# Indirect gathers on GpSimd: a fixed order, and a wait for the predecessor's landing before every fourth

## The chip, the cores and the metric

The kernel runs on one core of one Trainium2 chip. The metric is the device time of one execution in microseconds, as the median of plain executions (without the profiler). Three such runs of the kernel before gave 609.22, 614.84 and 617.77 us.

## The reference

Two layers of a graph network over 4096 nodes with 64 features, with a 0/1 adjacency matrix of 4096 x 4096 whose entries are 1 with probability 0.00195, about eight in a row. Cut to what matters:

```python
# layer 0: hyperbolic aggregation over a node's neighbours
h = max(layernorm(x), 0)
w = adj / max(adj.sum(axis=1), 1e-8)
log_ij = logmap(h_i, h_j)             # Poincare ball: Mobius addition, arctanh of its norm
agg = einsum("ij,ijc->ic", w, log_ij)
x = x + expmap(0, agg @ W0 + b0)      # a tanh of the norm
# layer 1: neighbours weighted by their place in the row
h = max(layernorm(x), 0)
rank = cumsum(adj != 0, axis=1); deg = rank[:, -1:]
k = min(deg, 100); pos = rank - (deg - k)
wt = mask * where(pos > 0, 0.5 ** (k - pos), 0)
x = x + wt @ (h @ W1) + b1
```

Layer 0 needs a function of both nodes for each edge, so the features of each neighbour have to be fetched; layer 1 is a matrix product whose weights fall by half with each neighbour counted from the end of the row.

## The kernel before

The 4096 rows are 32 blocks of 128 (one row a partition), in four quarters of eight blocks. The whole adjacency matrix is read once, in 256 loads of 128 x 512 numbers (256 KB each) on the queue of SyncE (`load`, line 795). TensorE transposes each piece (line 799), ScalarE writes it as an 8-bit mask into SBUF (line 801), and TensorE multiplies the mask with powers of two to pack 16 columns into one word (`pack`, line 822).

From the packed words VectorE finds the column numbers of a row's neighbours: `search` (lines 843 and 845) takes the largest 24 words of a row, `ell_lists` (line 866) turns the first eight into the row numbers `ell_i`. What doesn't fit into eight goes to a short list for the whole block, made by `tail_split`, `tail_first` and `tail_second`, which ends in `tail_i` (line 973): two entries for each partition and block.

Layer 0 is done on 16 units of two row blocks. A table in HBM, `tab_d`, has one row of 65 numbers (260 bytes) for each node: a scale and its 64 features. It is written once near the start (line 760). For a unit, `gather` (line 987) issues 16 indirect DMAs for two blocks of eight neighbours, and, for 12 of the units, 4 or 6 more for `tail_i`. One such DMA (line 995, called a gather below) takes 128 row numbers, one for each partition, and fetches 128 table rows into one of the 22 columns of the buffer `g`. There are 256 + 64 = 320 gathers. They are issued by GpSimd, which does nothing else after the first microseconds. The buffer `g` comes from the pool `gp`, which has two: the gathers of a unit can start when the unit two before it has finished with its own.

What uses a unit's buffer, in this order: `differ` subtracts the row's own features (VectorE, lines 1038, 1045 and 1053) and squares (ScalarE, line 1060, back into `g`); `weigh` sums the squares (VectorE, line 1072, the last reader of `g`) and computes the weight of each edge in small operations on VectorE and ScalarE; `total` adds up the weighted differences (line 1117 and following, with TensorE products at line 1107 for tail entries). When the units of a group of row blocks are done, `middle` (four steps) does layer 0's product, tanh and layer norm, and layer 1's product `h @ W1`, into `sup`. Groups are 8, 8, 8, 6 and 2 blocks.

Layer 1's weights come from `ranks` (lines 1223 to 1231): two matrix products on the mask count the neighbours to the right, and ScalarE's Exp turns the counts into powers of two, in place of the mask. `collect` (line 1246) multiplies these weights with `sup`, and VectorE reduces and adds the result (lines 1254 and 1258). `write` sends the output out.

All of this is written as a plan: each piece is given a due time by hand, and the pieces are handed to a scheduler in that order. Gathers are planned at 1.26 us each:

```python
took = 1.26 * (E2 + (u["tail"][1] * TB if u["tail"] else 0))
t = start + took
at(u_fetch, fetch, u)
at(start, gather, u)
```

From the due times as priorities, and from modelled times at which inputs become ready, the scheduler lays out one fixed list of instructions for each engine when the program is built. It also adds the semaphore waits. An engine works its list in order: an instruction that waits holds up those behind it. The gathers count their landing on eight semaphores, in turn; a gather thus waits for the one eight before it. At the end a flag tells whether any list was too short; a second, dense path would then run (it doesn't with these inputs).

Of the kernel before, what the change touches and what calls it, by code (L numbers as in the profile page):

```python
# [53 lines left out]
SUB = 40  # L54
REST = 64
TB = 2
MAXT = 3
ROW1 = 4096.0

# [479 lines left out]
def kernel(  # L539
# [27 lines left out]
    nc = tc.nc  # L567
# [8 lines left out]
    GB = P // GRP  # L576
    NSL = 2 * ELL + MAXT * TB
    SB = 4
# [12 lines left out]
    def by_rows(t):  # L591
        return t.rearrange("(b p) c -> p b c", p=P)

    with ExitStack() as fast:
# [26 lines left out]
        rest = const.tile([P, P], BF16, name="rest_b")  # L621
# [34 lines left out]
        ell_i = const.tile([P, NB, ELL], I32, name="ell_i")  # L656
        tail_i = const.tile([P, NB, TB], I32, name="tail_i")
        tail_r = const.tile([P, NB, TB], F32, name="tail_r")
        acc = const.tile([P, NB, D], F32, name="acc")
# [120 lines left out]

        EARLY = {"middle":30,"search":30,"fetch_words":30,"tail_rows":30,"differ":30,"weigh":30,"total":30,"total_tail":30,"ell_lists":30,"tail_split":20,"tail_first":20,"tail_second":20,"gather":30,"fetch":30}
        st = {}

        groups = [(0, 8), (8, 8), (16, 8), (24, 6), (30, 2)]

# [157 lines left out]
        def tail_second(q):  # L943
# [21 lines left out]
            nc.vector.transpose(lt, tb)  # L965
            lv = lt.rearrange("p (s t n b) -> p s n b t", s=2, t=TB, n=2)
            li = lst.tile([P, QB, TB], I32, name="li")
            for n in range(2):
# [9 lines left out]
        def fetch(u):  # L978
# [3 lines left out]
            if u["tail"]:  # L982
                t0, nt = u["tail"]
                u["hr"] = hr = blk.tile([P, MAXT, 3 * DT], BF16, name="hr")
                nc.scalar.dma_start(out=hr[:, 0:nt, :], in_=by_rows(hp_d)[:, t0 : t0 + nt, :])

        def gather(u):
            rb = u["ell"]
            g = u["g"] = gp.tile([P, NSL, DT], F32, name="g")
            idx = [ell_i[:, rb + b, s : s + 1] for b in range(2) for s in range(ELL)]  # L990
            if u["tail"]:
                t0, nt = u["tail"]
                idx += [tail_i[:, t0 + b, t : t + 1] for b in range(nt) for t in range(TB)]
            for k, i in enumerate(idx):
                nc.gpsimd.indirect_dma_start(  # L995
                    out=g[:, k, :],
                    out_offset=None,
                    in_=tab_d,
                    in_offset=bass.IndirectOffsetOnAxis(ap=i, axis=0),
                )  # L1000
            u["ns"] = len(idx)

        def tail_rows(u):
# [4 lines left out]
            nb = nt * TB  # L1008
            oh = u["oh"] = blk.tile([P, MAXT * TB, P], BF16, name="oh")
            row = tail_r[:, t0 : t0 + nt].rearrange("p b t -> p (b t)")  # L1010
# [5 lines left out]
            )  # L1016
            mp = ps_m.tile([P, MAXT * TB, P], BF16, name="mi")
            for k in range(nb):
                nc.tensor.transpose(mp[:, k, :], oh[:, k, :], ident_b)
            mt = blk.tile([P, MAXT * TB, P], BF16, name="mt")  # L1020
            nc.scalar.copy(mt[:, 0:nb], mp[:, 0:nb])
            sel = u["sel"] = ps_s.tile([P, MAXT * TB, DT], F32, name="sel")
            for k in range(nb):
# [280 lines left out]
        for n, u in enumerate(units):  # L1304
            lists = u["ell"] + 2 if u["ell"] < QB else (u["ell"] // 4 + 1) * 4
            start = max(t, loaded(lists - 1) + 6.0)
# [4 lines that stand above are left out]
            z = start + SH  # L1311
            u_fetch = z + 3.0
            at(z, tail_rows, u)
            at(z + 1.0, differ, u)
            at(z + 4.0, weigh, u, 0)
            at(z + 5.0, weigh, u, 1)
            at(z + 6.0, weigh, u, 2)
            at(z + 7.0, total, u)
            at(z + 8.0, total_tail, u)
            for k, (m, z0) in enumerate(todo):  # L1320
                at(max(z, TLOADED + 4.0 + 12.0 * m) + z0, middle, m, k % 4)
            todo = []
            for m, (g0, nb) in enumerate(groups):
                if u["tail"] and m not in ready and g0 + nb <= sum(u["tail"]):

                    todo += [(m, z0) for z0 in (1.5, 4.5, 5.5, 7.5)]
                    ready[m] = t + 30.0
# [69 lines left out]
```

## Time and profile before

| | |
|---|---|
| plain executions, median of three | 614.84 us (609.22 to 617.77) |
| profiled execution | 873.66 us |
| its span, first to last instruction | 871.5 us |
| gathers on GpSimd (line 995) | 320, 0.94 us each in most cases, starts 1.25 us apart in a row of them |
| first gather, last gather start | 56.9 us, 757.9 us |
| packets of the gathers' DMA queue | 10240, 8.8% of 16 DMA engines' time |
| adjacency loads | 256 of 256 KB |
| mean granted TensorE clock | 0.73 |

The profiled execution is 42% longer than the plain ones. Every time of an instruction below is from the profiled execution, and the prediction says how it gets from one to the other. In the profile's lines, L995 is line 995 of the kernel; PE is TensorE's products and PEld its weight loads, DVE is VectorE, ACT ScalarE, POOL GpSimd, SP SyncE, and a q behind an engine's name means its queue of DMA issues. "a<-b" means that tile a is computed from tile b. An arrow behind an idle time names what ended it; "issue" means that nothing in the profile explains the wait, and "remote" that a semaphore's update was seen but not whose it was.

### The profile page before, as it was taken

To read this page: it belongs to the slowest core of one execution; us is meant where nothing else is said; L and a number is where in the kernel's file an instruction comes from. 1 tells how busy PE (TensorE), PEld (TensorE's weight loads), DVE (VectorE), ACT (ScalarE), POOL (GpSimd) and SP (SyncE) were. 2 spreads that over 40 slices of the span, in tenths; PEclk is the share of its full clock that TensorE was granted. 3 is DMA by queue.
4 is the path that set the end of the run, shared out by engine and by line. 5 is a ranking of instruction groups with operands and counts; after the bars stand their busy time and mean duration, and the time that the engine had idled before them with its cause. 6 is when DMAs were issued, how large, how long until landed. Compare 5 with 4: busy or idle time off the path is not lost.

```text
span 871.5 us, 11735 instructions
## 1 busy us (share of the span) xinstructions
PE 481.0 (55%) x4170; PEld 317.3 (36%) x4170; DVE 408.2 (47%) x1494; ACT 354.1 (41%) x550; POOL 319.4 (37%) x332
## 2 busy tenths in 40 slices
PE   3654346276116628382553717655663199569894
PEld 2421124144003315151432404222422088359783
DVE  4550216356201627262542705844581054389786
ACT  3543237286006628281653806834481023022100
POOL 0035761604770441547053170555367502600000
PEclk9995557688557858586675966958695589578886
DMA  7899447387225647483563722211212100100002
GB/s 213 241 168 135 111 120 208 97 247 201 49 50 181 193 91 240 102 239 67 177 180 95 240 57 52 35 25 30 38 31 27 23 20 16 24 6 8 2 3 51
DMA packets 85590, 89.19 MB, mean 102 GB/s; under 512 B 46098, under 2 KB 47634, under 8 KB 85522
## 3 DMA queue, kind: packets, MB, share of 16 engines
q1 hardware_dynamic: 66194, 74.93, 31.6%
q0 software_dynamic: 10240, 10.67, 8.8%
q10 hardware_dynamic: 9088, 2.75, 1.4%
q8 instruction: 34, 0.56, 0.3%
q14 instruction: 34, 0.28, 0.1%
HBM read 84.12 MB, written 4.19 MB: 101 GB/s over the span
## 4 chain that ended last, share of the span: by engine, by line
PE 26%; another core or an unknown queue 22%; DMA 21%; issue 11%; DVE 10%; ACT 8%; SPq 2%; ACTq 0%; DVEq 0%
DMA a_sb<-in_adj 20%; PE a_ps L1246 8%; PE a_ps L799 5%; ACT mask L1231 3%; PE t L1227 3%; PE t L1223 3%; ACT mask L801 2%; DVE red L1254 2%; PE sel L1107 2%; PE words L1141 2%; SPq L795 1%; DVE acc L1258 1%; ACT g L1060 1%; PE o L1137 1%
## 5 line engine op out<-in xcount | busy, mean ns | idle before, releaser
L995 POOL DMA_INDIRECT g<-tab_d,ell_i x256 | 255.2, 997 | 406.2 <-DVE d L1072 124.8
L1231 ACT ACTIVATE mask<-t,w_c 128x512 fp8e5<-128x512 f32 x256 | 172.7, 691 | 205.3 <-remote 122.6
L1223 PE MATMUL t<-mask,rest_b 128*128 128x512 fp8e4 x248 | 114.3, 461 | 141.8 <-ACT mask L1231 101.7
L801 ACT ACTIVATE mask<-a_ps 128x1024 fp8e4<-128x1024 bf16 x128 | 131.2, 1028 | 138.1 <-remote 88.8
L799 PE MATMUL a_ps<-ident_b,a_sb 128*128 128x128 bf16 x1024 | 127.0, 263 | 94.6 <-DMA a_sb<-in_adj 68.5
L799 PEld LDWEIGHTS <-a_sb 128*128 128x128 bf16 x1024 | 79.8, 116 | 158.4 <-DMA a_sb<-in_adj 111.6
L1227 PE MATMUL t<-mask,before 128*128 128x512 fp8e4 x256 | 119.1, 465 | 1.8 <-issue 1.7
L1246 PE MATMUL a_ps<-sup,mask 128*128 128x192 bf16 x1024 | 109.6, 267 | 15.8 <-issue 9.8
L1246 PEld LDWEIGHTS <-mask 128*128 128x128 fp8e5 x1024 | 95.6, 106 | 29.5 <-issue 24.0
L1227 PEld LDWEIGHTS <-before 128*128 128x128 bf16 x256 | 27.4, 107 | 167.5 <-issue 165.5
L822 PE MATMUL words<-pk,mask 128*128 128x8 bf16 x1024 | 47.3, 169 | 59.7 <-issue 30.5
L822 PEld LDWEIGHTS <-mask 128*128 128x128 fp8e4 x1024 | 44.0, 104 | 92.1 <-issue 49.5
L995 POOL DMA_INDIRECT g<-tab_d,tail_i x64 | 62.4, 976 | 32.6 <-issue 18.9
L843 DVE MAX8 cand<-wsb 128x8 f32<-128x256 f32 x96 | 36.9, 416 | 68.7 <-ACT wsb L833 44.7
L1254 DVE TENSOR_REDUCE red<-a_ps 128x128 f32<-128x384 f32 x64 | 35.6, 556 | 26.2 <-PE a_ps L1246 17.9
L1223 PEld LDWEIGHTS <-rest_b 128*128 128x128 bf16 x248 | 28.0, 113 | 19.1 <-issue 10.6
L1072 DVE TENSOR_REDUCE d<-g 128x22 f32<-128x1408 f32 (+2 forms) x16 | 23.8, 1485 | 22.0 <-ACT g L1060 14.8
L1141 PE MATMUL words<-w_sb,a_sb 64*128 64x64 f32 x128 | 23.8, 339 | 17.2 <-issue 15.8
L1038 DVE TENSOR_TENSOR d<-g,hi 128x1024 f32<-128x1024 f32 x16 | 19.4, 1215 | 28.0 <-DMA g<-tab_d,ell_i 27.9
L1138 ACT COPY a_sb<-o 64x512 f32<-64x512 f32 (+1 forms) x18 | 9.5, 529 | 53.5 <-remote 18.1
L1141 PEld LDWEIGHTS words<-w_sb,a_sb 64*128 64x128 f32 x128 | 21.0, 243 | 24.1 <-issue 19.7
L1137 PE MATMUL o<-ident,y 128*64 128x128 f32 x64 | 14.2, 357 | 24.3 <-issue 12.8
(285 smaller groups left out, 535.0 us busy)
## 6 DMA issues: line engine op xcount, KB each, us to landing
a_sb<-in_adj SPq DMA_DIRECT2D x256, 256.0 KB
g<-tab_d,ell_i POOLq DMA_INDIRECT x256
hp_d<-mask SPq DMA_DIRECT2D x1, 1560.0 KB
hr<-hp_d ACTq DMA_DIRECT2D x8, 146.2 KB
tab_d<-mask SPq DMA_DIRECT2D x1, 1040.0 KB
hi<-tab_d ACTq DMA_DIRECT2D x16, 64.0 KB
g<-tab_d,tail_i POOLq DMA_INDIRECT x64
out<-acc SPq DMA_DIRECT2D x8, 128.0 KB
```

The lines of the kernel that those rows point to most:

```text
L799: nc.tensor.transpose(a_ps[:, m, k, :], upper[:, bass.ts(k, P)], ident_b)
L801: nc.scalar.activation(masks[q][:, 2 * SB * n : 2 * SB * n + 2 * SB, bass.ts(b, P)], a_ps.rearrange("p m k f -> p (m k) f"), AF.Copy, satu ...
L822: nc.tensor.matmul(words[:, rb % 2, bass.ts(j, GB)], lhsT=masks[q][:, j, bass.ts(b, P)], rhs=pk, start=False, stop=True, skip_group_check= ...
L843: nc.vector.max(out=top, in_=src)
L995: nc.gpsimd.indirect_dma_start(out=g[:, k, :], out_offset=None, in_=tab_d, in_offset=bass.IndirectOffsetOnAxis(ap=i, axis=0),)
L1072: nc.vector.tensor_reduce(d2, u["g"][:, 0:ns, 1:DT], AX.X, ALU.add)
L1141: nc.tensor.matmul(sp[:, k, :], lhsT=ht[:, bass.ts(k, P)], rhs=w_sb, start=True, stop=True)
L1223: nc.tensor.matmul(t, lhsT=rest, rhs=masks[p][:, j + 1, bass.ts(n, SW)], start=False, stop=False, skip_group_check=True,)
L1227: nc.tensor.matmul(t, lhsT=before, rhs=masks[p][:, j, bass.ts(n, SW)], start=(j == NB - 1), stop=True, skip_group_check=True,)
L1231: nc.scalar.activation(masks[p].bitcast(F8W)[:, j + 1, bass.ts(n, SW)], t, AF.Exp, bias=w_c, scale=-LN2, saturate=False,)
L1246: nc.tensor.matmul(o[:, k, :], lhsT=masks[p].bitcast(F8W)[:, b0 + j + 1, bass.ts(2 * n + k, P)], rhs=st["sup", c][:, j, :], start=(j == 0) ...
L1254: nc.vector.tensor_reduce(red, o.rearrange("p k (n c) -> p k c n", n=3), AX.X, ALU.add)
```

## The change

Each gather is tied to the one issued before it, across units. Three of four ties give an order only. The fourth, before gathers number 4, 8, 12 and so on, counted from 0 over the whole kernel, makes the gather wait until the one before it has landed in SBUF.

```diff
 TB = 2
+RUN = 4
...
         st = {}
+        runs = []
+        landed = mybir.DependencyInfo(
+            mybir.DependencyClass.Sync, mybir.DependencyReason.DATA
+        )
+        queued = mybir.DependencyInfo(
+            mybir.DependencyClass.NoSync, mybir.DependencyReason.DATA
+        )
...
             for k, i in enumerate(idx):
-                nc.gpsimd.indirect_dma_start(
+                ins = nc.gpsimd.indirect_dma_start(
                     out=g[:, k, :],
                     out_offset=None,
                     in_=tab_d,
                     in_offset=bass.IndirectOffsetOnAxis(ap=i, axis=0),
                 )
+
+                if runs:
+                    dep = landed if len(runs) % RUN == 0 else queued
+                    tc.add_manual_dep(ins.ins, runs[-1], dep, reason="rest")
+                runs.append(ins.ins.name)
             u["ns"] = len(idx)
```

`Sync` edges become semaphore waits; `NoSync` edges only fix the order in the list. Since the scheduler sees the waits when it lays out the lists, the order of instructions on the other engines can change too.

## The prediction

> **What bounds the kernel now.** I read the page first: span, busy shares, GpSimd's slices and the chain that ended last.
>
> ```profile
> span 871.5 us, 11735 instructions
> PE 481.0 (55%) x4170; PEld 317.3 (36%) x4170; DVE 408.2 (47%) x1494; ACT 354.1 (41%) x550; POOL 319.4 (37%) x332
> ...
> PE 26%; another core or an unknown queue 22%; DMA 21%; issue 11%; DVE 10%; ACT 8%; SPq 2%; ACTq 0%; DVEq 0%
> ...
> L995 POOL DMA_INDIRECT g<-tab_d,ell_i x256 | 255.2, 997 | 406.2 <-DVE d L1072 124.8
> ...
> L995 POOL DMA_INDIRECT g<-tab_d,tail_i x64 | 62.4, 976 | 32.6 <-issue 18.9
> ```
>
> No engine is full and the 320 gathers of line 995 are not on the chain. But 22% of the chain has no known releaser, and this execution took 873.7 us where plain ones took 614.8. So I asked what is different in it. Busy time by stretch (columns: length, then busy us and instructions of PE, PEld, DVE, ACT, POOL, then clock, DMA share, GB/s), cut where gathers run (205:261, 293:319) and pause:
>
> ```profile
> 172.00:205.00 33.00, 23.12 (x230) 13.33 (x230) 19.05 (x81) 25.56 (x37) 0.02 (x1) 0.81 0.76 222
> 205.00:261.00 56.00, 13.95 (x129) 7.78 (x128) 12.66 (x50) 10.61 (x14) 42.90 (x44) 0.59 0.38 85
> 261.00:293.00 32.00, 20.56 (x242) 12.90 (x241) 13.05 (x48) 23.82 (x36) 0.00 (x1) 0.80 0.65 199
> 293.00:319.00 26.00, 8.60 (x67) 4.35 (x63) 9.15 (x44) 6.37 (x11) 19.25 (x20) 0.59 0.40 94
> ...
> 759.00:871.50 112.50, 85.29 (x752) 75.39 (x751) 87.73 (x304) 14.66 (x38) 0.00 (x0) 0.76 0.06 14
> ```
>
> Under the profiler TensorE issues 230 matmuls in 33 us without gathers and 129 in 56 us beside them. The list of waits shows where ScalarE lost that time, and what GpSimd waited for (total us, times, longest):
>
> ```profile
> ACT mask L1231 <- remote: 122.6, 20, 18.8
> ACT mask L801 <- remote: 88.8, 14, 20.7
> ...
> POOL g L995 <- DVE d L1072: 124.8, 4, 41.6
> POOL g L995 <- issue: 95.6, 302, 3.9
> ...
> POOL g L995 <- DMA g<-tab_d,ell_i: 8.1, 5, 4.5
> ```
>
> With the two smaller entries of the same kind (18.1 and 14.3 us) ScalarE's waits of unknown origin sum to 243.8 us; 871.5 - 243.8 = 627.7 us, close to the plain 614.8. I read it so: most of these stalls belong to the profiled execution, and a plain one is that execution without them. Then GpSimd's 288.8 us of waiting between bursts (all its waits but issue and the first one, for tab_d) shrinks with them. GpSimd's timeline gives its pace:
>
> ```profile
> 79.15 0.94 POOL L995 DMA_INDIRECT g<-tab_d,ell_i  x1 [4.51 <-DMA g<-tab_d,ell_i]
> 82.74 0.94 POOL L995 DMA_INDIRECT g<-tab_d,ell_i  x1 [2.65 <-DMA g<-tab_d,ell_i]
> ...
> 226.36 0.94 POOL L995 DMA_INDIRECT g<-tab_d,ell_i  x1 [0.31 <-issue]
> 227.60 0.94 POOL L995 DMA_INDIRECT g<-tab_d,ell_i  x1 [0.30 <-issue]
> 228.85 0.94 POOL L995 DMA_INDIRECT g<-tab_d,tail_i  x1 [0.30 <-issue]
> ```
>
> Starts are 1.25 us apart (0.94 and 0.30), so 320 gathers are 400 us of GpSimd's time. The first starts at 56.9 us, and 112.5 us follow the last. 57 + 400 + 112.5 + 2.2 (873.7 - 871.5, outside the span) = 571.7; the plain 614.8 leaves GpSimd 43 us of waiting. By this sum the gathers pace a plain run, though the profiled chain hides it.
>
> **What the Trainium skill says.** "DMA: Bandwidth & Descriptors", section "Anatomy of one DMA — SWDGE (gpsimd) path", gives a GpSimd DMA a fixed cost of about 2.0 us, most of it the confirmation that the last byte has landed. The trace agrees: from a gather's start to the last of its recorded semaphore updates I count 2.09 us at least, 2.45 median, 3.0 mean (worst 16, while the first loads crowd the queues). "Perfetto Trace Analysis", section "Per-instruction lifecycle: what the profiler-reported window actually captures", says that such an instruction's profiled end is the end of descriptor generation and that GpSimd is better timed by the spacing of starts; hence 1.25 us and not 0.94.
>
> **The change part by part.** *Fixed order.* In the timeline the gathers already run unit by unit, 16 by ell_i and then 4 or 6 by tail_i; one place differs (18 ell_i starts from 204.98 on, before the six tail_i: two gathers of unit 5 go ahead of unit 4's tail). Swapping those costs about nothing, since unit 4's tail rows start right behind without a wait. *The ordering edges* add no instruction.
>
> *The waits.* Gathers 4, 8, ... 316 wait until the one before has landed: 79 waits. Today the gathers count on eight semaphores, 40 each, and gather n waits for gather n-8; that is almost always over (8.1 us in all, 5 times). The new wait is never over: the predecessor started only 1.25 us earlier and needs 2.45. Restart after a landing is 0.26 us (in the two rows at 79.15 and 82.74 the semaphore's last update is at 78.89 and 82.48). So each wait costs 2.45 + 0.26 - 1.25 = 1.46 us; from below, with the shortest landing, 2.09 + 0.26 - 1.25 = 1.10; from above, with the mean, 2.0. It can't be below nothing, as no landing seen is under 1.25 us. Times 79: 115 us, between 87 and 158. A run of four takes 6.5 us instead of 5.0, a unit of 22 some 8 us more.
>
> Behind a waiting gather stand only gathers. For them wait VectorE's differ (lines 1038 and 1045), then ScalarE's square (1060), VectorE's sum (1072), weigh, total, middle and, last, collect. VectorE, ScalarE and TensorE also hold loads' transposes, ranks and collects behind these in their fixed queues, so lateness spreads.
>
> *What covers it.* In the profiled execution, 288.8 us of GpSimd waits lie between bursts, so most of 115 us can hide there: 873.7 us plus 0 to 115, less whatever shorter stalls give back. In a plain run the cover is the 43 us alone, mostly waits for a free g buffer (pool gp has two), which slower gathers do absorb. With all of it: 614.8 + 115 - 43 = 687 us. None absorbed gives 730. Later gathers also leave VectorE (87.7 us busy in the last 112.5) less left over from before: with nothing left over the last unit's differ, at 787.8, would start 2.4 us after the last gather, and 86 us would follow that gather instead of 112.5; this gives 661. I take the middle of 687 and 661, 674 us. With the shortest tail and the cheapest waits, 57 + 400 + 87 + 86 + 2.2 = 632.
>
> *The rest.* Instructions of the other engines are the same, but their order is laid out at build time from modelled readiness, which the waits shift. No row prices that; I take nothing, with some 15 us either way inside the range.
>
> **Rivals.** *Hidden (no change).* The plain spacing of gathers may be less than the profiled 1.25. With 0.95 (0.30 of issue gone) gathers are 304 us, slack 139, and waits 79 x (2.45 + 0.26 - 0.95) = 139: 615 us. For it: GpSimd is not on the profiled chain. Against: each of several hundred spacings is 1.25, and all slack would have to lie where the waits fall.
>
> *Rest heals the stalls (faster).* The first stall comes some 10 us into a burst (burst from 112.06, TensorE idle from 122), as if something filled up; a pause after every fourth gather may let it drain. If a plain run keeps a share of the 243.8 us and the pauses clear it, GpSimd's own path decides: with spacing 0.95 it is 57 + 304 + 139 + 86 = 586 us. It decides only where stall time saved exceeds the waits not covered, and at 1.25 spacing the floor of 632 rules it out. For it: the threefold slowdown beside gathers. Against: 627.7 against 614.8, which leaves plain runs hardly any stall.
>
> *The waits don't do what they say:* if they were satisfied already, as the eight-semaphore waits are, 615 us; the landing times speak against it, and I count it with no change.
>
> **How the numbers follow.** Likeliest, waits on the pacing path: 0.76, 674 us, its own range 632 to 735. No change: 0.12, 615. Stalls heal: 0.12, 586. The range reaches down to 606, taking in most of no change and leaving out healing, and up to 735, with some 0.06 above. Faster by over 2% 0.12, within 2% 0.12, slower by over 2% 0.76; 2% is about what a measurement of this kernel tells from no change.
>
> **What would show it.** Right: GpSimd's timeline has groups of four starts 1.25 us apart, then a start some 2.7 us after its predecessor with a DMA of g as releaser; about 79 such waits of 1.2 to 1.7 us beyond the 0.30; plain time up by 45 to 115 us. Wrong: gaps before every fourth gather near 0.30; or plain time unchanged with the gaps there (GpSimd had slack); or, beside gathers, matmuls and GB/s near those of stretches without, and plain time down (stalls are real in plain runs, and rest clears them).

## The result, and the profile after

The changed kernel takes 761.7 us (760.1 to 765.2) against 614.84 us: 1.242 times the time before, 95% interval 1.226 to 1.257. Forecast were 674 us, 606 to 735. The direction and the place were right, the size was not. The page of the kernel after, whose profiled execution took 760.1 us, as long as its other runs:

```profile
span 758.2 us, 11815 instructions
PE 474.9 (63%) x4170; PEld 320.3 (42%) x4170; DVE 414.5 (55%) x1494; ACT 357.2 (47%) x550; POOL 331.5 (44%) x332
...
L1003 POOL DMA_INDIRECT g<-tab_d,ell_i x256 | 265.3, 1036 | 302.9 <-DMA g<-tab_d,ell_i 162.6
...
L1003 POOL DMA_INDIRECT g<-tab_d,tail_i x64 | 64.4, 1007 | 55.8 <-DMA g<-tab_d,tail_i 22.1
...
g<-tab_d,ell_i POOLq DMA_INDIRECT x256, 2.9
```

The gathers (line 1003 now) are as many as before and about as long (1.04 us in the mean for those by `ell_i`, 1.00 before). What ended GpSimd's idle time has changed: the landing of a gather instead of a result of VectorE. The last line is the median from issue to landing, 2.9 us. The list of waits (total us, times, longest):

```profile
POOL g L1003 <- DMA g<-tab_d,ell_i: 181.6, 63, 13.7
...
POOL g L1003 <- issue: 84.1, 241, 4.3
...
POOL g L1003 <- DMA g<-tab_d,tail_i: 22.1, 8, 5.5
```

There are 71 waits on a landing with 203.7 us, where there were 5 with 8.1; ScalarE's waits of unknown origin are gone from the list. GpSimd's timeline (start, length, idle before):

```profile
206.31 1.50 POOL L1003 DMA_INDIRECT g<-tab_d,ell_i  x1 [3.45 <-DMA g<-tab_d,ell_i]
208.11 0.94 POOL L1003 DMA_INDIRECT g<-tab_d,ell_i  x1 [0.30 <-issue]
209.35 0.94 POOL L1003 DMA_INDIRECT g<-tab_d,ell_i  x1 [0.30 <-issue]
210.60 0.94 POOL L1003 DMA_INDIRECT g<-tab_d,ell_i  x1 [0.30 <-issue]
214.52 0.94 POOL L1003 DMA_INDIRECT g<-tab_d,ell_i  x1 [2.98 <-DMA g<-tab_d,ell_i]
```

Groups of four as foreseen, but the start at 214.52 comes 3.92 us after its predecessor, not 2.7. Over all 79 waits that spacing is 3.89 us in the mean.

The earlier profile of the kernel before had stalls that the plain runs lacked, so one experiment took a second one (first below). Against it the whole difference can be read from GpSimd's row alone. The table splits the span of each profiled execution at the starts of the first and the last of the 320 gathers; the first column of times is the median time of the kernel, in the first row that of one execution. Two runs on the old lists, with the waits two back and with the waits on the gather itself, are not in it, since their profiled executions were over 1% longer than the median of their others.

| kernel | median us | ratio to before | to first gather | first to last | after last | span |
|---|---|---|---|---|---|---|
| before, again | 610.9 | | 55.7 | 459.2 | 93.9 | 608.8 |
| after | 761.7 | 1.242 | 55.7 | 634.2 | 68.3 | 758.2 |
| old lists, 79 waits | 816.9 | 1.315 | 57.6 | 665.2 | 92.0 | 814.8 |
| new lists, no waits | 667.6 | 1.075 | 57.2 | 529.8 | 80.0 | 667.0 |
| order only | 627.2 | 1.011 | 58.0 | 461.0 | 107.3 | 626.3 |
| old lists, four back | 628.5 | 1.012 | 57.4 | 472.3 | 94.1 | 623.8 |
| old lists, every eighth | 716.7 | 1.162 | 56.4 | 563.1 | 94.5 | 714.0 |
| old lists, first half | 721.7 | 1.170 | 57.4 | 568.5 | 93.8 | 719.7 |
| old lists, second half | 702.3 | 1.138 | 57.2 | 554.2 | 92.1 | 703.5 |
| new lists, every eighth | 691.1 | 1.120 | 56.4 | 557.8 | 75.9 | 690.1 |
| new lists, wait on gather | 741.6 | 1.204 | 57.2 | 613.5 | 67.3 | 738.0 |

"Lists" are the fixed orders of instructions on the engines. They did change: of VectorE's 1,494 instructions in the two traces, 944 at most can be read in the same order in both. So the change has two parts, the waits and the new lists, and the experiments separate them. After against before: 175.0 us more from first to last gather, 25.6 us less behind the last, 149.4 in all.

### The profile page after: what moved, and what is told of

Read it like the earlier page. It is cut to its first block, busy times and chain, and to the rows that moved or that the text cites. A ratio compares the mean times of both kernels' runs of the same rounds, so it can differ in the third digit from the quotient of the medians.

```text
span 758.2 us, 11815 instructions
## 1 busy us (share of the span) xinstructions
PE 474.9 (63%) x4170; PEld 320.3 (42%) x4170; DVE 414.5 (55%) x1494; ACT 357.2 (47%) x550; POOL 331.5 (44%) x332
## 5 line engine op out<-in xcount | busy, mean ns | idle before, releaser
L1003 POOL DMA_INDIRECT g<-tab_d,ell_i x256 | 265.3, 1036 | 302.9 <-DMA g<-tab_d,ell_i 162.6
L807 PE MATMUL a_ps<-ident_b,a_sb 128*128 128x128 bf16 x1024 | 120.6, 255 | 97.9 <-DMA a_sb<-in_adj 95.5
L807 PEld LDWEIGHTS <-a_sb 128*128 128x128 bf16 x1024 | 75.0, 113 | 151.0 <-DMA a_sb<-in_adj 138.4
L1259 PE MATMUL a_ps<-sup,mask 128*128 128x192 bf16 x1024 | 105.8, 268 | 32.3 <-DVE red L1267 21.5
L1240 PE MATMUL t<-mask,before 128*128 128x512 fp8e4 x256 | 117.3, 458 | 0.2 <-ACT mask L1244 0.2
L1003 POOL DMA_INDIRECT g<-tab_d,tail_i x64 | 64.4, 1007 | 55.8 <-DMA g<-tab_d,tail_i 22.1
L1240 PEld LDWEIGHTS <-before 128*128 128x128 bf16 x256 | 27.3, 107 | 94.5 <-issue 91.7
L1073 ACT ACTIVATE g<-d 128x1408 f32<-128x1408 f32 (+2 forms) x16 | 20.3, 1270 | 92.6 <-DVE d L1066 75.3
L1236 PEld LDWEIGHTS <-rest_b 128*128 128x128 bf16 x248 | 28.2, 114 | 19.2 <-issue 9.9
L1154 PE MATMUL words<-w_sb,a_sb 64*128 64x64 f32 x128 | 26.3, 365 | 14.0 <-DVE y L1189 10.6
L1154 PEld LDWEIGHTS words<-w_sb,a_sb 64*128 64x128 f32 x128 | 23.3, 268 | 21.1 <-issue 12.5
L1120 PE MATMUL sel<-d,mr 128*128 128x65 f32 x128 | 22.8, 344 | 12.6 <-DVE mr L1115 12.6
```

The costliest lines, as they stand in the source:

```text
L807: nc.tensor.transpose(a_ps[:, m, k, :], upper[:, bass.ts(k, P)], ident_b)
L1003: ins = nc.gpsimd.indirect_dma_start(out=g[:, k, :], out_offset=None, in_=tab_d, in_offset=bass.IndirectOffsetOnAxis(ap=i, axis=0),)
L1120: nc.tensor.matmul(ag[:, k // TB, :], lhsT=mr[:, k, :], rhs=d[:, E2 + k, :], start=(k % TB == 0), stop=(k % TB == TB - 1),)
L1154: nc.tensor.matmul(sp[:, k, :], lhsT=ht[:, bass.ts(k, P)], rhs=w_sb, start=True, stop=True)
L1236: nc.tensor.matmul(t, lhsT=rest, rhs=masks[p][:, j + 1, bass.ts(n, SW)], start=False, stop=False, skip_group_check=True,)
L1240: nc.tensor.matmul(t, lhsT=before, rhs=masks[p][:, j, bass.ts(n, SW)], start=(j == NB - 1), stop=True, skip_group_check=True,)
```

## The experiments

Theory A is that the waits pace GpSimd, and GpSimd the program. Theory B is that the new lists cost most of it.

**The kernel before once more**, with no edit.

> The kernel before once more, unchanged, for its profile. The prediction took some 244 us of ScalarE stalls in the earlier profiled execution (873.7 us against a median of 614.8) for something that belongs to that execution. If they come with every profiled execution of this kernel, this one shows a span near 870 us again. If they were that execution's alone, the span is 615 to 630 us, like the plain runs and like the profiles of the two experiments with gathers in unbroken bursts (626.3 and 623.8 us).

It took 610.9 us. Its page, and its list of waits:

```profile
span 608.8 us, 11735 instructions
...
PE 444.2 (73%) x4170; PEld 300.1 (49%) x4170; DVE 407.5 (67%) x1494; ACT 353.7 (58%) x550; POOL 336.0 (55%) x332
...
DMA 32%; POOL 22%; PE 17%; DVE 15%; issue 10%; ACT 3%; SPq 0%; DVEq 0%; ACTq 0%; POOLq 0%
```

```profile
POOL g L995 <- issue: 92.1, 302, 0.3
POOL g L995 <- DMA tab_d<-mask: 53.2, 1, 53.2
POOL g L995 <- ACT mask L1231: 19.5, 2, 19.2
POOL g L995 <- DMA g<-tab_d,ell_i: 8.4, 5, 3.5
```

The chain's 22% of unknown origin has gone and POOL stands there with 22%. The stalls belonged to that one execution, as the prediction took it; what caused them there stays open. GpSimd waits for nothing of weight after its first gather except 19.2 us ahead of unit 4. (The list puts these down to ScalarE's line 1231. The trace fits another reading better: VectorE has written the unit's row numbers, line 866, at 166.41 us, and the gather starts at 167.15; the buffer had been free since 147.34. In the run below the row numbers are written at 217.32 and the gather starts at 218.06, again 0.74 us later.)

**Old lists with the waits.** The waits are put in after the lists are laid; in the trace all 1,494 instructions of VectorE stand in the order of the kernel before. This sketch and those below show the core of each edit.

```diff
 # kernel before, instruction lists already fixed; k counts the gathers
+for k in range(4, 320, 4):
+    gather[k].waits.append(landing of gather[k - 1])
```

> The kernel before with the instruction lists of all five engines kept exactly as they are, and only the waits added: every fourth of the 320 gathers (79 of them) also waits until the gather ahead of it has landed. Nothing of the computation is left out. Theory A (the waits alone pace GpSimd: about 2.64 us more at each of 79 waits, 209 us, plus 27 us of slower ordinary starts, less about 86 us of cover): 745 to 790 us, like the changed kernel, with gaps of some 3.9 us from start to start at the waits. Theory B (the newly laid lists of VectorE, ScalarE and TensorE cost most of the 147 us): 650 us or less. My prediction's own price (1.46 us each, 43 us of cover) would give about 675 us.

816.9 us, ratio 1.315 (1.304 to 1.326). Theory B is out: the waits alone cost more than the whole change. It is also 27 us above the top of theory A's range. Two causes came out later: each restart took 0.74 us here, and the stretch behind the last gather stays at 92 us.

**New lists without the waits.**

```diff
 # kernel after, instruction lists already fixed
+for k in range(4, 320, 4):
+    move the wait for gather[k - 1] from gather[k] to gather[k + 7]
```

> The changed kernel with its instruction lists kept exactly as they are, and only the waits taken off: the wait for the landing of gather k-1 that each of 79 gathers k carries is moved to gather k+7, where the eight semaphores in turn ask for it anyhow. Nothing of the computation is left out. Theory A (waits): 600 to 660 us, near the kernel before. Theory B (newly laid lists): 700 to 762 us. If it lies between, both have a share, and with the run of the old lists with waits the shares can be read off.

667.6 us, ratio 1.075 (1.065 to 1.085), a little over theory A's range: the new lists cost 46 us of their own when the waits are not there. That alone is more than the 15 us that the prediction allowed for them. GpSimd's waits in this run:

```profile
POOL g L1003 <- DVE u L1086: 45.2, 4, 24.5
POOL g L1003 <- DVE ta L941: 36.4, 2, 20.4
POOL g L1003 <- DVE d L1085: 11.2, 2, 10.2
```

VectorE's list was laid with the waits in view; without them GpSimd waits for VectorE, 92.8 us in these three lines. The two effects don't add up: old lists plus waits is +195 us, new lists plus waits +147.

**Order only.**

```diff
-    dep = landed if len(runs) % RUN == 0 else queued
+    dep = queued
```

> The changed kernel with the fixed order of the gathers kept and no waits at all (each gather is tied to its predecessor in the list, none waits for a landing); the scheduler lays the lists itself from these ties. Nothing of the computation is left out. Theory A: 605 to 625 us, as before. Theory B: the lists are neither those of before nor those of after, so anything from 615 to 700 us. If the fixed order by itself costs something, it shows here as more than 630 us. I expect that in its profiled run ScalarE's and TensorE's long stalls of the kernel before are there again, since the gathers go in unbroken bursts.

627.2 us, ratio 1.011 (1.003 to 1.019), just above theory A's range: the fixed order costs at most a per cent or two. The stalls that I expected in its profile were not there (span 626.3).

**The same places, four back.**

```diff
+    gather[k].waits.append(landing of gather[k - 4])
```

> The kernel before with its lists kept, and about 79 waits added at the same places as in the changed kernel, but each for the landing of the gather four ahead instead of the one just ahead. Nothing of the computation is left out. With starts 1.25 us apart, the gather four ahead has been started 5 us earlier and lands after about 2.9 us, so the wait is over when it is reached. Theory A in its form 'it is the landing that is waited for': 610 to 635 us. If a wait costs by being there (an extra semaphore instruction, a restart of the descriptor work) it is 79 times 0.5 us, up to 40 us more than that, less what cover there is. Theory B: 615 us.

628.5 us, ratio 1.012 (1.009 to 1.015). Being there costs a wait next to nothing; waiting costs.

**Two back.**

```diff
+    gather[k].waits.append(landing of gather[k - 2])
```

> The kernel before with its lists kept and 79 waits at the same places, each for the landing of the gather two ahead. Nothing of the computation is left out. If a wait costs what is left of landing plus restart when it is reached: 3.51 + 0.75 = 4.26 us after the start of the gather two ahead, where 2.5 us pass anyhow, so 1.76 us each, 139 us, less the cover that the runs with waits on the predecessor showed (79 times 3.17 = 250 us of waits made the stretch of gathers 193 us longer than with harmless waits: 57 us): 700 to 720 us. If the cost is in having only one gather under way at a time, and two are enough to hide the landing: 630 to 660 us.

719.5 us, ratio 1.166 (1.155 to 1.176), at the top of the first range. A wait costs what is left of landing and restart when it is reached; having two gathers under way is not enough to hide it.

**The wait on the gather itself.** A gather with several waits keeps the first on itself; the others go to a semaphore instruction ahead of it. On the old lists 78 of the 79 waits for a landing had gone there; here none does.

```diff
-    gather[k].waits.append(landing of gather[k - 1])
+    gather[k].waits.insert(0, landing of gather[k - 1])
```

> The kernel before with its lists kept and the same 79 waits for the predecessor as in the run of the old lists with waits (817 us), but the wait for the predecessor is put first among a gather's waits, so that it sits on the gather itself; the wait for the semaphore's reuse, long over, goes to the separate semaphore instruction ahead of it. Nothing of the computation is left out. There the gather started 0.74 us after the landing, in the changed kernel 0.26 us wherever the wait sat on the gather. If the place of the wait sets the restart: 79 times 0.48 = 38 us less, 770 to 790 us. If the restart is the same wherever it sits: 805 to 825 us.

778.2 us, ratio 1.261 (1.249 to 1.273), 39 us less than with the other placing, or some 33 us by the two ratios, since the two were not timed beside the same runs of the kernel before. The same on the lists of the changed kernel, where only 39 gathers needed it:

> The changed kernel as it is, lists and waits kept, except that in the 39 gathers whose wait for the predecessor sits on a separate semaphore instruction it is put on the gather itself (0.26 instead of 0.74 us from landing to start). Nothing of the computation is left out. If the restarts add up as on the old lists (38 us for 79): 39 times 0.48 = 19 us less than the changed kernel, a ratio to the kernel before of 1.20 to 1.22, where the changed kernel had 1.242. If the new lists hide the restart: 1.235 to 1.25.

741.6 us, ratio 1.204 (1.196 to 1.212), 20 us under the changed kernel's median (23 by the ratios). Restart from landing to start, from the trace: 0.26 us on the gather, 0.74 us on the separate instruction (mean 0.52 in the changed kernel, 0.26 here). Its list of waits shows the same, 168.7 us in 61 waits (2.77 each) beside 181.6 in 63 (2.88, half of them already at 0.26):

```profile
POOL g L1003 <- DMA g<-tab_d,ell_i: 168.7, 61, 12.0
```

The changed kernel lies half-way between the two placings (39 gathers of one kind, 40 of the other). Half-way between the two runs on old lists is 1.288; the changed kernel has 1.242. The new lists thus give back 0.046 times 617 = 28 us when the waits are there, give or take some 11 by the intervals. The two runs with every wait on the gather say it without a half-way: 1.261 on the old lists, 1.204 on the new, 35 us. The stretch behind the last gather shows where. Windows of the second profile of before, of old lists with 79 waits, and of after (length, then busy us of PE, PEld, DVE, ACT, POOL):

```profile
514.90:608.80 93.90, 71.72 (x622) 62.80 (x622) 75.21 (x262) 11.77 (x34) 1.21 (x1) 0.77 0.07 15
```

```profile
722.70:814.80 92.10, 72.06 (x622) 63.09 (x622) 73.15 (x252) 11.20 (x32) 0.94 (x1) 0.78 0.07 16
```

```profile
689.90:758.20 68.30, 39.91 (x294) 33.32 (x294) 49.52 (x182) 7.73 (x23) 0.94 (x1) 0.62 0.08 18
```

On the old lists 622 matmuls follow the last gather however late it is, since the order is fixed; in the changed kernel 328 of them come ahead of it, into the gaps.

**Half as many waits**, on old lists:

```diff
-for k in range(4, 320, 4):
+for k in range(8, 320, 8):
```

> The kernel before with its lists kept and half as many waits: every eighth gather (39 of them) waits for the landing of its predecessor. Nothing of the computation is left out. With a price of 3.17 us each (from the run with 79) and a cover of 57 us that is spent first: 124 - 57 = +67, so 680 to 700 us. If each wait costs in proportion (195 us over 79 waits = 2.47 us, no cover): +96, 710 to 725 us. With the prediction's price of 1.46 and 43 us of cover: 57 - 43 = +14, 630 to 640 us.

716.7 us, ratio 1.162 (1.154 to 1.171), inside the range for no cover and above mine. The trace says why it isn't that: landings were longer here, 3.84 us in the mean against 3.51 with 79 waits, so 39 waits make 39 x (3.84 + 0.74 - 1.25) = 130 us, and the stretch of gathers grew by 103.9: 26 us were covered. With 79 waits it is 79 x (3.51 + 0.74 - 1.25) = 237, and 206.0 of growth: 31 covered. The cover exists, is about 30 us (from one execution each), and 39 waits spend nearly as much of it as 79.

And with the lists laid anew for these waits:

```diff
-RUN = 4
+RUN = 8
```

> The changed kernel with every eighth gather waiting instead of every fourth (39 waits), the lists of the other engines laid anew by the scheduler for these waits. Nothing of the computation is left out. The same waits on the old lists cost 99 us. If lists that are laid with the waits in view give back some 28 us, as between the old lists with 79 waits and the changed kernel: 680 to 700 us. If they give back nothing here: 710 to 725 us.

691.1 us, ratio 1.120 (1.111 to 1.128): 26 us under the old lists, of which 18.6 are behind the last gather (75.9 for 94.5).

**Waits in one half only.**

```diff
-for k in range(4, 320, 4):
+for k in range(4, 152, 4):      # first half; range(152, 320, 4) in the second
```

> The kernel before with its lists kept; only the waits of the first 152 gathers are added (37 of them, units 0 to 7), every fourth for its predecessor, the wait placed as in the run of the old lists with all 79. Nothing of the computation is left out. In that run unit 8 started 116 us later than in the kernel before. If GpSimd paces the program from first to last gather and has no slack, these 116 us stay: 725 to 745 us. If later stretches have the slack that the prediction called cover (43 us), it takes them back: 680 to 700 us.

> The kernel before with its lists kept; only the waits of the gathers from 152 on are added (42 of them, units 8 to 15). Nothing of the computation is left out. In the run with all 79, this stretch grew by 76 us, with landings of 2.75 us in the middle once the big loads are through, against some 4 us beside them. No slack: 690 to 705 us, and this half plus the first half make the 195 us of the whole. With 43 us of slack here: 645 to 660 us. If the price of a wait were the same early and late, the 42 of 79 would cost 104 us: 722 us.

721.7 us (ratio 1.170, 1.162 to 1.179), just below its range, and 702.3 us (ratio 1.138, 1.130 to 1.145), inside. The halves cost 105 and 86 us and together 191, where the whole cost 195: nothing later takes back what an early wait costs. A wait in the first half costs 105/37 = 2.8 us, in the second 86/42 = 2.0. The landings of the changed kernel agree, for those gathers whose landing the view can tell: line 1003 from 100 to 300 us, beside loads of some 240 GB/s, and from 400 to 650, at some 30 GB/s:

```profile
DMA to landing us min/median/max: 2.9/3.8/5.7
```

```profile
DMA to landing us min/median/max: 2.3/2.6/3.7
```

The other profiles agree: between 300 and 450 us the median landing was 2.7 to 3.0 us in the seven kernels that moved 86 to 118 GB/s there, 3.2 us in one at 130, and 3.4 to 3.8 us in the five on old lists that still moved 159 to 184. That the loads lengthen the landing is read from this; a run without the loads wasn't made. None of the kernels beat the one before.

## Why the prediction was wrong in size

**Right: the plain kernel is the profiled one without the stalls, and GpSimd paces it.** The second profile has neither the stalls nor the long waits between bursts. On the old lists every change of the gathers' stretch came out in the span: 103.9 us in 105.2 with 39 waits, 206.0 in 206.0 with 79.

**Off in its terms: the plain path of 57 + 400 + 112.5 + 2.2.** The second profile has 55.7 + 459.2 + 93.9. The sum with the 43 us came out right because the 43 us were what it lacked. The gathers take 60 us more than 319 times 1.25, since some starts are slower and units wait at their beginning, and the stretch behind the last is 19 us shorter.

**Near in size by luck: the cover of 43 us.** In the changed kernel the 79 waits hold 208.9 us over the 1.25 spacing, the other starts 26.6; before, all starts held 60.5. So 208.9 + 26.6 - 60.5 = 175.0 us of growth, and 34 us covered. But 43 was about what two errors left, 60 us too little in the gathers and 19 too much behind them. And the reason given, waits for a free g buffer, is not the one seen: that line is 2.9 us (VectorE's d, line 1072) in the second profile. What was covered is mostly older delay in the same places: of the 60.5 us before, 31.1 were at the same 79 starts, 18.9 of them ahead of unit 4, and there a wait for a landing took the place of the older delay instead of adding to it. On the old lists 15.8 us of the wait ahead of unit 4 are still there, only later.

**Wrong: the price of a wait.** This is the step that failed: "So each wait costs 2.45 + 0.26 - 1.25 = 1.46 us". Measured in the changed kernel is 3.37 + 0.52 - 1.25 = 2.64 us, 209 us for 79 instead of 115. The landing is 0.92 us longer, for two reasons. I put a median into a sum that needs the mean (2.86 and 3.37 for these 79). And both figures, 2.45 and the mean of 3.0, came from a record with holes: a gather raises its semaphore 16 times (281 of the 320 gathers of the second profile show exactly 16), but the stalled profile holds 1,017 of these 5,120 updates, about three for each gather, and the last of three recorded can come before the landing. The second profile of the same kernel holds 5,047, and there the landing is 3.7 us in the median and 3.9 in the mean. The holes may not be all of it: thinned at random to as few updates as the first, the second profile still gives 3.3 and 3.6 (an estimate), so part may belong to the stalled execution itself, and that stays open. A price from the second profile, with its 3.98 us at the same 79 places, would have been 2.99 us, somewhat too high: 165 of its gathers start before 300 us, beside the loads, and only 108 of the changed kernel's. The Trainium skill's fixed cost of about 2.0 us ("DMA: Bandwidth & Descriptors", "Anatomy of one DMA — SWDGE (gpsimd) path") is near the shortest landing of the changed kernel, 2.33 us; it is no price for a wait beside loads, where the measured mean decides. The restart is 0.26 us longer, because half of the waits sit on a separate instruction; the two rows that I took it from had the wait on the gather.

**Half right: the end.** I weighed 112.5 us behind the last gather against 86 and took the middle, -13 us. It is -25.6. It doesn't come by itself, as I argued, from VectorE having less left over: on old lists it stays at 92 to 94 us. It comes from the new lists, for which I had taken nothing: 80.0 us with the new lists alone, 68.3 with the waits too.

The sum as predicted: 115 - 43 - 13 = +59. As measured: 209 - 34 - 26 = +149, all of the difference between the two spans (the 34 is what the gathers' stretch leaves, so that the sum closes by itself; the 209 and the 26 are read).

**The rivals.** No change: the spacing of starts is 1.25 us (median) in the second profile too, so there was no hidden slack. Rest heals the stalls: plain runs have none to heal (its sum, 586, also left out the 2.2 us outside the span). Waits that are over when they are reached: the 71 waits on a landing rule it out. A rival that the prediction didn't name is TensorE's granted clock, 0.78 in the changed kernel and 0.86 in the second profile of the kernel before. GpSimd's waits account for the growth of the gathers' stretch without it, and behind the last gather the old lists take 92.1 us with the waits and 93.9 without, at a clock of 0.78 and 0.77.

## What to carry to other kernels

A wait for the transfer just issued costs its landing and restart less the time between issues; add up means, taken beside the traffic that will run there and from a record that holds all the updates, not the median of another state. Look further back instead: the same 79 waits cost 195 us one gather back, 102 two back and about 7 four back. When a scheduler lays the lists with a wait in view, take the wait and the lists apart before saying what either costs: here the new lists cost 46 us alone and gave some 30 us back with the waits.

## What the runs showed of the hardware that was not expected

- Landing to start of the next gather is 0.26 us when the wait sits on the gather and 0.74 us when it sits on a separate semaphore instruction ahead of it; moving the wait onto the gather was worth 33 to 39 us in 79 gathers.
- In the changed kernel a gather lands in 2.6 us (median) once the big loads are through, and in 3.8 us beside loads of some 240 GB/s.
- One profiled execution of an unchanged kernel can be 873.7 us where another is 610.9 and the plain runs are 609 to 618. The first held a fifth of the semaphore updates of the gathers, 1,017 of 5,120, the second 5,047. Only the second showed which waits were the kernel's, and how long a landing takes.
